# A graph network's gathered rows: the sums of pairs in a tile of their own instead of in place

## The chip, the cores and the metric

One Trainium2 chip, one core of it. The metric is the device time of one execution in microseconds (us); an execution takes about 4.4 ms, so that 0.3% are 13 us. The engines are TensorE (PE for matmuls, PEld for its weight loads), VectorE (DVE), ScalarE (ACT), GpSimd (POOL) and SyncE (SP). The engines run side by side, each through its own list of instructions in order, and wait for one another through semaphores.

## The reference, cut to what matters

Two graph networks follow each other on 3125 nodes and 103125 edges, in float32. The second has three attention layers of 256, 256 and 128 features, and only in these does the change act:

```python
def _gat(x, src, dst, W, a_src, a_dst, bias, n_nodes):
    H, C = a_src.shape
    xw = (x @ W).reshape(n_nodes, H, C)
    al_s = jnp.einsum('nhc,hc->nh', xw, a_src)
    al_d = jnp.einsum('nhc,hc->nh', xw, a_dst)
    logits = jax.nn.leaky_relu(al_s[src] + al_d[dst], LRELU_SLOPE)
    m = jax.lax.stop_gradient(jax.ops.segment_max(logits, dst, num_segments=n_nodes))
    e = jnp.exp(logits - m[dst])
    denom = jax.ops.segment_sum(e, dst, num_segments=n_nodes)
    alpha = e / denom[dst]
    out = jax.ops.segment_sum(alpha[:, :, None] * xw[src], dst, num_segments=n_nodes)
    return out.reshape(n_nodes, H * C) + bias
```

Each node sums the feature rows of its neighbours, each row weighted for each of the H = 8 heads.

## The kernel before

A search at the start sorts a node's edges into two kinds. Part of them is met by one-hot matrices (at most one edge for each block of 125 source nodes), the rest by gathering rows from a table in memory with indirect DMAs. For one attention layer `gat` first projects the features (L1107) and writes the table `tab`. Then `add_edges` sums over the edges, and `close_rows` joins both kinds of sums, normalizes and applies the activation. `add_edges` is written under a manual schedule: every engine takes its instructions in the order in which the Python code issues them, and nothing is reordered.

Its main loop goes over NT = 25 tiles of nodes. In pass `t` it works on two tiles at once, with two streams of edges.

The one-hot stream. For tile `t + 1`, `gather` (L1146) issues PE matmuls that look rows up with the one-hot matrix `hot` (L1152), two lookups to a PSUM pair `g`, of which there are two; ACT copies each pair to SBUF (L1153) and calls `pump()`. For tile `t`, `add_part` (L1190) multiplies the rows with the weights on DVE (`times`, L1188), adds the second half of the rows to the first on DVE (L1195), and PE sums the rest in PSUM with matmuls against the identity (L1197). ACT copies the sum out (L1303). `weigh` (L1174) makes the weights of the next tile from L1178 to the sum in `exps` (L1326), with the exponential on ACT (L1325).

The stream of gathered rows. A tile `t` has MORE[t] columns of gathered edges, one row for each of its 128 nodes in each column: 44 in the first tile, then 24, 22, 21, 20, 19, 18, 17, 17 and so on down to 7. The generator `fetches` fetches them column by column (L1021, an indirect DMA that POOL issues) into tiles `rows` of up to SG = 8 columns, a group each, with BUFS = 6 buffers. It is driven by `pump`: each ACT copy of a lookup pair lets one or two fetches go, and before the first of them ACT writes a few bytes into the row (L1221), which holds POOL back until ACT is there. `sum_others` takes a tile whose rows have been fetched long enough ago: `weigh_others` (L1255) makes its weights, again with the exponential on ACT, and `add_others` (L1266) sums it. In `add_others` DVE weights a group (L1188), adds its second half to its first, in place (L1272), and PE sums what is left in PSUM (L1274). With an odd number of columns the middle one is left as it is. ACT copies the sum out (L1280), and POOL scatters it to memory later (L1013).

In one pass the order on DVE is therefore: the two large parts of `add_part`, the logits of `weigh_others` and its exponential's sum, the small third part (`last`), the groups of `add_others`, and `weigh` for the next tile. Of the tile pools that matter here, `io` has two buffers for a name unless `bufs` says otherwise.

Of the kernel before, what the change touches and what calls it, by code (L numbers as in the profile page):

```python
# [10 lines left out]
F32 = mybir.dt.float32  # L11
# [8 lines left out]
P = 128  # L20
# [25 lines left out]
MORE = (44, 24, 22, 21, 20, 19, 18, 17, 17, 16, 16, 15, 15, 14, 14, 13, 13, 13, 12, 11, 11, 10, 10, 8, 7)  # L46
# [5 lines left out]
SG = 8  # L52
# [570 lines left out]
class Fast(Base):  # L623
# [510 lines left out]
    def add_edges(self, io, ps, layer, D, xt, yt, xw, ald, stat, tab, ald_d, res, more):  # L1134

        nc = self.nc
# [49 lines left out]
        def times(rows, e, s0, n):  # L1186
            r = rows[:, :n, :D].rearrange("p k (h c) -> p k h c", c=C)
            nc.vector.tensor_tensor(r, r, e[:, s0 : s0 + n, :, None].to_broadcast([*r.shape[:3], C]), op=ALU.mult)  # L1188
# [55 lines left out]
        def sum_others(ripe):  # L1244

            nonlocal held
            weighed = None
            while queue and queue[0][0] <= ripe:
                if weighed:
                    end_others(*add_others(*weighed))  # L1250
                weighed = weigh_others(*queue.pop(0)[1])
                held -= len(weighed[1])
            return weighed
# [12 lines left out]
        def add_others(t, groups, e, o):  # L1266
            pa = ps.tile([P, D], F32, name="pa2", tag="pa2")
            for rows, k0, n in groups:
                times(rows, e, k0, n)
                m = (n + 1) // 2  # L1270
                if n > 1:
                    nc.vector.tensor_add(rows[:, : n - m, :D], rows[:, : n - m, :D], rows[:, m:n, :D])  # L1272
                for k in range(m):
                    nc.tensor.matmul(  # L1274
                        pa, self.ident, rows[:, k, :D], start=k0 + k == 0, stop=k0 + n == MORE[t] and k == m - 1
                    )
            return t, o, pa

# [11 lines left out]
        for t in range(NT):  # L1290
            ahead = t + 1 < NT
            if t + 2 < NT:
                load(t + 2)
            nxt = parts(t + 1) if ahead else []
            pa = ps.tile([P, D], F32, name="pa1", tag="pa1")[:Q]
            for i in range(3):
                if ahead:
                    gather(t + 1, *nxt[i])
                if i == 2:
                    weighed = sum_others(copies - 8)  # L1300
                add_part(pa, e, *now[i])
            o = io.tile([P, D], F32, name="o1")[:Q]
            nc.scalar.copy(o, pa)  # L1303
            by_rows(nc.scalar, res[t * Q : (t + 1) * Q], o)
            added = weighed and add_others(*weighed)
            if ahead:
                now, e = nxt, weigh(t + 1, nxt)
            if added:
                end_others(*added)
        while queue or fetching.gi_frame:  # L1310
            for i in range(2 * SG):
                send(False)
            weighed = sum_others(copies)
            if weighed:
                end_others(*add_others(*weighed))
# [183 lines left out]
```

## Time and profile before

| | us |
|---|---|
| runs, median of 3 | 4444.06 |
| runs, lowest and highest | 4442.77, 4454.39 |
| the profiled execution | 4467.44 |
| its span, first to last instruction | 4465.6 |
| DVE products of gathered rows (L1188, `rows`) | 293.1 busy, x180 |
| POOL gathers (L1021, `rows`) | 1252.5 busy, x1200 |
| PE lookups (L1152, `hot`) | 584.8 busy, x2400 |

The page of a profile counts, for each engine, busy time, its share of the span and the instructions. A group line names line, engine, operation, what is written and what is read, the shapes (partitions x elements), the count, then busy time, mean ns of one, and the idle time of the engine just before such instructions with what ended most of it. A float32 matmul of this kernel stands in the trace as two passes, so that counts of PE are twice those in the code. The granted TensorE clock of the profiled execution was 0.753 of full speed on average. In the timeline a row is start, length, engine, line, operation, and in brackets the idle time before it and what ended that.

### The profile page before, as it was taken

The numbers are of one execution on the slowest core, as the hardware profiler recorded it, in microseconds if no ns is written. First come the engines' busy times: TensorE is split into PE (matmuls) and PEld (weight loads), VectorE is DVE, ScalarE is ACT, GpSimd is POOL, SyncE is SP. The second block draws the span as 40 slices with busy tenths as digits, with TensorE's granted clock in tenths as the row PEclk, the third lists the DMA queues.
The fourth block names the chain that finished last, engine by engine and source line by source line (L and its number), as shares of the span: only waits on it lengthen the run. The fifth ranks groups of instructions, "written<-read, shape, count | busy, mean of one in ns | idle before, by whom it ended". The sixth has DMA issues, their size and how long they took to land. (4 is left out here: it accounts for less than half of the span.)

```text
span 4465.6 us, 33146 instructions
## 1 busy us (share of the span) xinstructions
PE 2415.4 (54%) x10021; PEld 1730.4 (39%) x10021; DVE 2197.9 (49%) x3553; ACT 941.2 (21%) x2618; POOL 2002.9 (45%) x1916
## 2 busy tenths in 40 slices
PE   0001620000499767777777577777776555555545
PEld 0000300000133345565555445555555444444445
DVE  6898842100000227767666436666765434434445
ACT  0001620000000232232222332222232322121112
POOL 4415056777200045576652045567662045565550
PEclk8555955555799878888888788888888776776676
DMA  3001869500599463444331463344341553333322
GB/s 115 12 11 38 286 169 267 165 0 1 202 358 366 175 168 119 122 129 141 119 107 44 123 173 110 116 122 149 120 120 33 126 116 97 85 88 93 87 68 58
DMA packets 224527, 558.02 MB, mean 125 GB/s; under 512 B 89262, under 2 KB 134710, under 8 KB 208496
## 3 DMA queue, kind: packets, MB, share of 16 engines
q1 hardware_dynamic: 112286, 307.88, 20.7%
q0 software_dynamic: 74800, 158.73, 14.9%
q10 hardware_dynamic: 37250, 89.18, 6.6%
q8 instruction: 82, 1.34, 0.1%
q14 instruction: 109, 0.89, 0.1%
HBM read 439.37 MB, written 116.25 MB: 124 GB/s over the span
## 5 line engine op out<-in xcount | busy, mean ns | idle before, releaser
L1021 POOL DMA_INDIRECT rows<-tab,idx x1200 | 1252.5, 1044 | 894.1 <-ACT rows L1221 396.2
L1152 PE MATMUL g<-xw,hot 125*125 125x264 f32 (+1 forms) x2400 | 584.8, 394 | 252.9 <-issue 142.2
L1153 ACT COPY xt<-g 125x528 f32<-125x528 f32 (+1 forms) x900 | 474.5, 530 | 795.5 <-PE g L1152 411.7
L1152 PEld LDWEIGHTS g<-xw,hot 125*125 125x125 f32 x2400 | 434.6, 212 | 380.4 <-issue 169.7
L1013 POOL DMA_INDIRECT adj<-val,celli x400 | 423.9, 1060 | 299.8 <-DMA x<-in_x 148.4
L1049 PE MATMUL pa<-adj_t,h 125*64 125x500 f32 (+1 forms) x1050 | 270.7, 552 | 511.8 <-DMA adj_t<-adj 511.1
L1274 PE MATMUL pa<-rows,ident 128*128 128x256 f32 (+1 forms) x1236 | 391.8, 495 | 204.8 <-DVE rows L1272 163.3
L1021 POOL DMA_INDIRECT at<-ald,perm x75 | 78.2, 1043 | 789.2 <-DMA gat_dense<-dense 438.7
L1188 DVE TENSOR_TENSOR xt<-xt,le 125x3072 f32<-125x3072 f32 (+1 forms) x150 | 421.8, 2812 | 0.0
L1274 PEld LDWEIGHTS pa<-rows,ident 128*128 128x128 f32 x1236 | 304.4, 288 | 295.3 <-DVE rows L1272 197.4
L1197 PE MATMUL pa<-xt,ident 125*125 125x256 f32 (+1 forms) x1800 | 385.6, 369 | 39.1 <-DVE xt L1195 37.6
L1326 DVE TENSOR_REDUCE o<-le 128x8 f32<-128x104 f32 (+16 forms) x75 | 21.9, 292 | 740.1 <-ACT le L1325 484.4
L1152 PE MATMUL g<-xw,xt 125*125 125x264 f32 (+1 forms) x1350 | 319.8, 389 | 122.3 <-ACT xt L1153 62.0
L1197 PEld LDWEIGHTS pa<-xt,ident 125*125 125x125 f32 x1800 | 323.8, 209 | 90.8 <-DVE xt L1195 26.3
L1049 PEld LDWEIGHTS pa<-adj_t,h 125*64 125x64 f32 x1050 | 86.2, 136 | 675.5 <-issue 578.1
L170 DVE TENSOR_TENSOR h<-p,L_gnn_b 125x256 f32<-125x256 f32 (+1 forms) x21 | 8.3, 396 | 649.6 <-PE p L168 649.6
L1152 PEld LDWEIGHTS g<-xw,xt 125*125 125x125 f32 x1350 | 240.4, 211 | 189.6 <-ACT xt L1153 96.7
L1188 DVE TENSOR_TENSOR rows<-rows,le 128x2048 f32<-128x2048 f32 (+8 forms) x180 | 293.1, 1629 | 0.0
L1195 DVE TENSOR_TENSOR xt<-xt 125x1536 f32<-125x1536 f32 (+1 forms) x150 | 223.7, 1491 | 4.9
L1197 PE MATMUL pa<-last,ident 125*125 125x256 f32 (+1 forms) x300 | 92.9, 444 | 207.4 <-DVE last L1188 167.9
L1061 ACT COPY gin_acc<-pa 128x500 f32<-128x500 f32 (+1 forms) x21 | 10.2, 532 | 771.9 <-DMA adj_t<-adj 524.0
L1272 DVE TENSOR_TENSOR rows<-rows 128x1024 f32<-128x1024 f32 (+5 forms) x174 | 157.0, 902 | 6.0
(272 smaller groups left out, 2838.0 us busy)
## 6 DMA issues: line engine op xcount, KB each, us to landing
hot<-hot SPq DMA_DIRECT2D x48, 1562.5 KB
adj_t<-adj SPq DMA_DIRECT2D x144, 500.0 KB
adj_t<-adj SPq DMA_DIRECT2D x72, 562.5 KB
xt<-hot SPq DMA_DIRECT2D x24, 1562.5 KB
adj<-a ACTq DMA_DIRECT2D x25, 1367.2 KB
hot<-one ACTq DMA_DIRECT2D x25, 1367.2 KB
rows<-tab,idx POOLq DMA_INDIRECT x1200
row<-lane_d SPq DMA_DIRECT2D x25, 683.6 KB
```

Of the source, the lines that this page charges most:

```text
L1013: st = self.nc.gpsimd.indirect_dma_start(out=table, out_offset=bass.IndirectOffsetOnAxis(ap=idx, axis=0), in_=row, in_offset=None)
L1021: self.nc.gpsimd.indirect_dma_start(out=out, out_offset=None, in_=table, in_offset=bass.IndirectOffsetOnAxis(ap=idx, axis=0))
L1049: nc.tensor.matmul(pa[i * D0 : (i + 1) * D0, c // B, :w], h[:, s], tiles[i][:, c : c + w], start=s0 == 0, stop=s0 + i >= NT - 2 and i == 1,)
L1061: nc.scalar.copy(acc[:, :w], pa[:, c // B, :w])
L1152: nc.tensor.matmul(g[:Q, j, :W], one, xw[:, t if s == NT else s], start=True, stop=True)
L1153: nc.scalar.copy(rows[:, i : i + 2], g[:Q, :, :W])
L1188: nc.vector.tensor_tensor(r, r, e[:, s0 : s0 + n, :, None].to_broadcast([*r.shape[:3], C]), op=ALU.mult)
L1195: nc.vector.tensor_add(rows[:, :m, :D], rows[:, :m, :D], rows[:, m:n, :D])
L1197: nc.tensor.matmul(pa, self.ident[:Q, :Q], rows[:, j, :D], start=s0 + j == 0, stop=s0 + n == NS and j == m - 1)
L1272: nc.vector.tensor_add(rows[:, : n - m, :D], rows[:, : n - m, :D], rows[:, m:n, :D])
L1274: nc.tensor.matmul(pa, self.ident, rows[:, k, :D], start=k0 + k == 0, stop=k0 + n == MORE[t] and k == m - 1)
L1326: nc.vector.reduce_sum(den, e.rearrange("p k h -> p h k"), axis=AX.X)
```

## The change

The sum of pairs goes to a new tile `two` of SG // 2 = 4 columns, and PE reads `two` instead of `rows`. Where a group has an odd number of columns, the one that has no partner is copied to `two` by DVE. `two` is taken from `io`, which gives it two buffers; it has 4 x 256 x 4 = 4096 bytes in each partition for a layer of 256 features.

```diff
             for rows, k0, n in groups:
                 times(rows, e, k0, n)
                 m = (n + 1) // 2
+                two = io.tile([P, SG // 2, D], F32, name="two")
                 if n > 1:
-                    nc.vector.tensor_add(rows[:, : n - m, :D], rows[:, : n - m, :D], rows[:, m:n, :D])
+                    nc.vector.tensor_add(two[:, : n - m], rows[:, : n - m, :D], rows[:, m:n, :D])
+                if n % 2:
+                    nc.vector.tensor_copy(two[:, m - 1], rows[:, m - 1, :D])
                 for k in range(m):
                     nc.tensor.matmul(
-                        pa, self.ident, rows[:, k, :D], start=k0 + k == 0, stop=k0 + n == MORE[t] and k == m - 1
+                        pa, self.ident, two[:, k], start=k0 + k == 0, stop=k0 + n == MORE[t] and k == m - 1
                     )
             return t, o, pa
```

In the program that is built from it, no engine's order changes apart from the 36 copies that DVE gets. The sums on DVE from the third group of a layer on carry a wait for PE, and the first fetch into a reused `rows` buffer waits for DVE where it waited for DVE and PE.

## The prediction

> **What bounds the kernel now.** I read the page first, then the busy time by stretch, the waits, the answers for lines 1272, 1274 and 1021, and last the timeline of one pass of the loop over `t`. The edit sits in `add_others`, which runs only inside `add_edges`: three stretches of the span, about 1600 to 2455 us, 2560 to 3400 us and 3600 to 4380 us.
>
> ```profile
> 1600.00:2455.00 855.00, 638.00 (x2380) 482.25 (x2379) 561.28 (x663) 243.59 (x681) 483.95 (x447) 0.84 0.40 114
> 2560.00:3400.00 840.00, 633.39 (x2332) 470.62 (x2331) 522.57 (x616) 245.34 (x684) 487.39 (x448) 0.86 0.43 125
> 3600.00:4380.00 780.00, 426.54 (x2288) 380.40 (x2288) 340.07 (x630) 159.18 (x655) 417.77 (x433) 0.71 0.33 83
> ```
>
> The columns after the length are PE, PEld, DVE, ACT and POOL busy. No engine is full: PE 75% in the first two stretches and 55% in the third, DVE 66, 62 and 44%, POOL 54 to 58%. So the time is a loop of handovers, and the question is which handover comes last.
>
> ```profile
> DVE o L1326 <- ACT le L1325: 484.4, 41, 23.8
> POOL rows L1021 <- ACT rows L1221: 396.2, 128, 40.0
> PE pa L1274 <- DVE rows L1272: 163.3, 67, 15.4
> DVE lle L1258 <- DMA rows<-tab,idx: 48.8, 7, 13.6
> ```
>
> These are waits (total us, times, longest). DVE's big wait is for the exponential of the gathered edges, which ACT takes behind its copies of PE's lookups; PE in turn waits for DVE's sums. DVE waits for gathered rows hardly at all: seven times named so, all on `lle`, which is tile 0 of a layer, where no `rows` buffer has been used before. One pass, with 19 gathered rows (groups of 8, 8 and 3), shows the loop:
>
> ```profile
> 1909.83 0.32 DVE L1326 TENSOR_REDUCE o<-le 128x8 f32<-128x152 f32 x1 [5.69 <-issue]
> ...
> 1914.25 6.78 PE L1274 MATMUL pa<-rows,ident 128*128 128x256 f32 x20 [2.33 <-DVE rows L1272]
> 1916.43 1.23 DVE L1272 TENSOR_TENSOR rows<-rows 128x1024 f32<-128x1024 f32 x1
> 1917.58 0.95 DVE L1188 TENSOR_TENSOR rows<-rows,le 128x768 f32<-128x768 f32 x1
> ...
> 1918.56 0.42 DVE L1272 TENSOR_TENSOR rows<-rows 128x256 f32<-128x256 f32 x1
> 1918.90 0.56 DVE L1178 TENSOR_TENSOR le<-xt,ald 125x96 f32<-125x96 f32 x2
> ...
> 1925.81 1.76 DVE L1195 TENSOR_TENSOR xt<-xt 125x1536 f32<-125x1536 f32 x1
> ...
> 1927.63 2.85 PE L1197 MATMUL pa<-xt,ident 125*125 125x256 f32 x12 [0.79 <-DVE xt L1195]
> ```
>
> From 1909.83 to 1927.6 DVE runs almost without a gap (0.40 us for one exponential), and at the end PE waits 0.79 us for it. Before 1909.83 DVE idled 5.69 us. So DVE time added between the sums and L1195 reaches PE in such a pass; in passes where PE is later, the next exponential wait swallows it.
>
> **The change, part by part.**
>
> *Removed: POOL's wait for PE.* Refilling a `rows` buffer now waits for DVE's sum or copy instead of PE's matmuls. What that wait costs is in the answer for line 1274:
>
> ```profile
> who waited for it (us, times):
> ...
>   POOL rows L1021: 16.8, 6
> ```
>
> 6 times, 16.8 us of 4465.6. And the rows fetched earlier are not awaited: after tile 1 of a layer DVE never waits for them. Tile 1's late gathers are not helped, because the first fetch into a reused buffer stands behind an ACT copy (L1221, at 1699.86 us) that ACT runs after L1280, which itself needs all of tile 0's matmuls. Value: 0; bounds 0 and -17 us. I take 0.
>
> *Moved: the output of L1272, and PE's operand.* The 174 sums keep their lengths (1226 ns for 1024 elements); only the destination differs, and is now contiguous. PE runs the same 1236 passes. In the program each of these matmuls waited for the DMA semaphore of its own row; now one wait on DVE a group is left, two where a copy follows. That is free already: in the trace the start-to-start of L1274's passes inside a group is 216 ns at full granted clock and 427 ns at half, exactly that of L1197, which has no such waits. Value 0.
>
> *Added: 36 DVE copies.* Groups of odd length: 12 of the 25 tiles end in one (21, 19, 17, 17, 15, 15, 13, 13, 13, 11, 11, 7 rows), times three layers; 24 copies of 256 elements and 12 of 128. No such copy is in the trace. From below: the 8-element copy of L1109, 167 ns. From above: the two-input sum of 256 elements (L1272, 425 ns) and of 128 (290 ns). The 3125-element one-input row (L1377, 1850 ns) runs at under 0.6 ns an element, so I put 0.53 ns an element on the 167: 300 ns and 235 ns. Sum: 24 x 0.300 + 12 x 0.235 = 10.0 us of DVE (bounds 6.0 and 13.7). Behind each copy stand `weigh(t+1)` and the products of L1188 and L1195, and PE waits for L1195. PE's own wait for the copied row is covered: that matmul is the tile's last, and 2 to 8 passes of 216 to 427 ns from earlier rows or groups are still running. Looking through the 36 places, PE next waits for L1195 within 12 us in about 10, all in the first two layers; there the 0.30 us goes on the path, 3 us. In the third layer DVE idles up to 23.8 us for the next exponential, which covers its copies.
>
> A rule speaks against these copies. The Trainium skill, "SBUF — State Buffer", section "Who interferes with whom", says that an fp32 SBUF-to-SBUF copy takes DVE's second port pair, shared with GpSimd, as an exclusive lock, and that whichever of the two comes second is blocked outright. POOL is issuing gathers (949 ns each) more than half of the time. By the rule a copy could wait up to one issue: 36 x 0.95 = 34 us at most. The nearest rows say less: L1007, a one-input DVE operation, ran from 588 to 843 us while POOL issued scatters (L1013, 579.6 to 1153.9 us), and its 25 took 1830/1850/2048 ns (min/median/max), against 1850 for the same length at L1377 with POOL idle. So at most 0.2 us on one copy, about 0 at the median. I take the row. The other direction, POOL behind a copy, is at most 0.3 us a copy on a queue that nobody is late for.
>
> *Added: DVE waits for PE.* `two` has two buffers, so each sum from the third group on waits until PE has summed the group two before. Across tiles this is long past, since PE must have finished the old tile before the lookups that feed the next exponential. Within a tile it matters from three groups on: 12 waits a layer, 36 in all. In the pass above PE starts group 1 at 1914.25; eight passes at half clock (427 ns) and a drain of 0.6 us end near 1917.9, and the third sum would start at 1918.56: margin 0.6 us. With a third group of one row (17 rows, six tiles) DVE is ready 3.8 us after PE starts, PE needs about 3.6 to 4.0: margin about 0. Going through all 36, the modelled matmul ends give negative margins of under 0.1 us in three places; semaphore records, which are incomplete, would allow some 8 us in all. I take 2 us on the path, bounds 0 and 8. Queued behind such a wait is again `weigh(t+1)`.
>
> Sum: 3 + 2 = +5 us, on 4467.4 for the profiled execution (span 4465.6), so 4472. The median of the runs, 4444.06, lies 23 us below the profiled one; the same 5 us give 4449. I put no factor on the difference.
>
> **Rivals.**
>
> *The ring of two becomes the wait (slower).* One mechanism: the third sum of a tile stands behind PE, and DVE with it. For: margins near zero, and PE is at half clock in most of L1274 (median matmul 421 ns, the shortest 274). Against: the waits that I could place are short. It decides from about 0.4 us a wait: 36 x 0.4 = 14 us when most are on the path. With all copies exposed too: 10 + 10 = +20, 4464 us.
>
> *Earlier gathers pay (faster).* If POOL's 16.8 us were on the path: 4444 - 17 = 4427 us. For: rows are released some 2.4 us earlier on average (an estimate: the end of PE's last pass of a group less the end of its sum). Against: no DVE wait for rows after tile 1.
>
> *It does nothing that counts.* POOL is paced by ACT's copies (396.2 us of waits) and by its own issue, not by PE; all 10 us of copies fall into exponential waits: 4444 us. It would read as no change too.
>
> **How the numbers follow.** Forecast, +0 to +13 us: 0.62, likeliest 4449. Nothing that counts, within some us of 4444: 0.12. The ring: 0.20. Earlier gathers: 0.06. The kernel's runs spread from 4442.8 to 4454.4, and 0.3%, 13.3 us, is about what a measurement of it can tell from no change. Low end 4437: the gather case, 0.06, lies below it. High end 4464, the ring's full price; what is beyond it, with the gather case, is less than 0.2. The first two layers do the same work in passes of differing lengths, but from the second copy of L1303 in a layer to its last they take 777 and 780 us, so I add nothing for chance reshuffling.
>
> **What would show it.** Copies of about 300 and 235 ns, 36 of them; if one takes over 0.5 us with POOL busy, the port rule holds. DVE before the new sum waiting for PE on the matmul line: under 3 us in all is my case, over 14 us the ring's. POOL's waits for PE's sums gone, with POOL's waits for ACT unchanged. PE's wait for L1195 up from 37.6 us by about 5. I am wrong if a stretch shrinks by more than 10 us, or if DVE's exponential waits don't absorb the copies of the third layer.

## The result, and the profile after

The changed kernel takes 4468.58 us (median of 20 runs, 4426.66 to 4490.33) where the kernel before, run beside it, takes 4442.84 us (20 runs, 4415.16 to 4457.47): a ratio of 1.0054, 95% interval 1.0036 to 1.0073, or +24 us (+16 to +32). It is slower, and the time lies above the predicted range of 4437 to 4464.

The profiled execution took 4472.63 us (span 4470.8), against 4467.44 before. Two single executions 5 us apart cannot show a difference of 24 us between medians: the runs of the two kernels spread over 42 and 64 us. So the traces are read here for what the edit does, and the size comes from the repeated runs.

The three stretches in the changed kernel's busy time, columns as before:

```profile
1600.00:2455.00 855.00, 650.64 (x2412) 489.49 (x2412) 564.59 (x676) 247.97 (x694) 485.23 (x450) 0.85 0.41 117
2560.00:3400.00 840.00, 634.84 (x2333) 470.70 (x2332) 525.87 (x630) 244.61 (x684) 487.75 (x448) 0.86 0.43 125
3600.00:4380.00 780.00, 424.12 (x2265) 375.36 (x2265) 335.74 (x637) 157.76 (x652) 415.39 (x432) 0.70 0.32 82
```

No stretch stands out; in the third, DVE got through 4 us less of its work than before. The lines of the changed kernel are three further down from L1274 on: the sum is L1273, the copy L1275, the matmul L1277, the exponential's sum L1329. The groups of sums and copies, with the idle time of DVE ahead of them behind the bar, the sum before first:

```profile
L1272 DVE TENSOR_TENSOR rows<-rows 128x1024 f32<-128x1024 f32 (+5 forms) x174 | 157.0, 902 | 6.0
...
L1273 DVE TENSOR_TENSOR two<-rows 128x1024 f32<-128x1024 f32 (+5 forms) x174 | 157.1, 903 | 24.8 <-remote 7.8 <-issue 0.5
L1275 DVE COPY two<-rows 128x256 f32<-128x256 f32 (+1 forms) x36 | 10.0, 278 | 8.5 <-remote 7.4 <-PE pa L1277 0.7
```

The sum itself costs what it did. Its idle time rose from 6.0 us to 24.8 us, and 8.5 us lie ahead of the copies. Two things make that up. The answers for lines 1273 and 1275 have the first:

```profile
L1273 DVEq EVENT_SEMAPHORE  x156: 21/21/21, 1691.3 to 4373.6; - x156
...
L1275 DVE COPY two<-rows x36: 219/286/501, 1866.0 to 4374.2; 128x256 f32<-128x256 f32 x24, 128x128 f32<-128x128 f32 x12
```

A sum that waits both for its product and for PE gets an instruction of its own for the second wait, between the product and the sum. Before, a sum began 34 ns (median) after its product ended; with that instruction between, 104 ns. 156 x 70 ns = 10.9 us of DVE.

The second is real waiting for PE: 2.5 and 5.3 us before two sums, 7.4 and 0.7 us before two copies, 15.9 us in all. (`remote` says that no instruction ended near the signal that the profile could name; the semaphore that these four wait for is raised by PE alone. The 0.5 us before one more sum are left out: the profile names no signal for them, and a like gap stands below in a kernel with a ring of four, put down to DVE's own product.) The longest, in the timeline (DVE and PE rows):

```profile
3940.86 4.00 PE L1277 MATMUL pa<-two,ident 128*128 128x128 f32 x16 [0.71 <-DVE two L1273]
...
3942.64 0.28 DVE L1188 TENSOR_TENSOR rows<-rows,le 128x128 f32<-128x128 f32 x1
3950.31 0.23 DVE L1275 COPY two<-rows 128x128 f32<-128x128 f32 x1 [7.39 <-remote]
...
3950.59 0.80 PE L1277 MATMUL pa<-two,ident 128*128 128x128 f32 x2 [5.74 <-issue]
```

PE's records of the earlier groups end at 3944.86, but DVE is let go at 3950.31 only. In between PE has no record. Whether its passes ended later than the trace models them, or only their signal came late, the trace doesn't tell; below, a stall of PE is such a gap. Before, DVE would have gone on to L1178 in that time. Now it stands in the queue behind PE, and PE's last two passes in turn wait for the copy.

### The profile page after: what moved, and what is told of

Same layout as the page of the kernel before. It is cut to its first block, busy times and chain, and to the rows that moved or that the text cites. A ratio compares the mean times of both kernels' runs of the same rounds, so it can differ in the third digit from the quotient of the medians.

```text
span 4470.8 us, 33080 instructions
## 1 busy us (share of the span) xinstructions
PE 2422.1 (54%) x10021; PEld 1731.1 (39%) x10021; DVE 2204.9 (49%) x3589; ACT 938.5 (21%) x2618; POOL 1998.5 (45%) x1916
## 5 line engine op out<-in xcount | busy, mean ns | idle before, releaser
L1021 POOL DMA_INDIRECT rows<-tab,idx x1200 | 1249.9, 1042 | 882.6 <-ACT rows L1221 495.6
L1152 PE MATMUL g<-xw,hot 125*125 125x264 f32 (+1 forms) x2400 | 582.6, 392 | 233.7 <-issue 131.4
L1152 PEld LDWEIGHTS g<-xw,hot 125*125 125x125 f32 x2400 | 429.4, 210 | 363.6 <-issue 162.1
L1277 PE MATMUL pa<-two,ident 128*128 128x256 f32 (+1 forms) x1236 | 388.6, 490 | 224.3 <-DVE two L1273 197.6
L1188 DVE TENSOR_TENSOR xt<-xt,le 125x3072 f32<-125x3072 f32 (+1 forms) x150 | 421.8, 2812 | 0.0
L1277 PEld LDWEIGHTS pa<-two,ident 128*128 128x128 f32 x1236 | 299.7, 284 | 314.5 <-DVE two L1273 208.8
L1197 PE MATMUL pa<-xt,ident 125*125 125x256 f32 (+1 forms) x1800 | 393.8, 375 | 43.3 <-DVE xt L1195 42.5
L1152 PE MATMUL g<-xw,xt 125*125 125x264 f32 (+1 forms) x1350 | 324.6, 393 | 116.7 <-ACT xt L1153 48.9
L1329 DVE TENSOR_REDUCE o<-le 128x8 f32<-128x104 f32 (+16 forms) x75 | 21.9, 291 | 697.8 <-ACT le L1328 413.1
L1152 PEld LDWEIGHTS g<-xw,xt 125*125 125x125 f32 x1350 | 244.6, 213 | 185.3 <-ACT xt L1153 80.2
L1188 DVE TENSOR_TENSOR rows<-rows,le 128x2048 f32<-128x2048 f32 (+8 forms) x180 | 293.2, 1629 | 0.0
L1195 DVE TENSOR_TENSOR xt<-xt 125x1536 f32<-125x1536 f32 (+1 forms) x150 | 223.7, 1491 | 4.9
L1273 DVE TENSOR_TENSOR two<-rows 128x1024 f32<-128x1024 f32 (+5 forms) x174 | 157.1, 903 | 24.8 <-remote 7.8
```

The source lines that it names most:

```text
L1021: self.nc.gpsimd.indirect_dma_start(out=out, out_offset=None, in_=table, in_offset=bass.IndirectOffsetOnAxis(ap=idx, axis=0))
L1152: nc.tensor.matmul(g[:Q, j, :W], one, xw[:, t if s == NT else s], start=True, stop=True)
L1195: nc.vector.tensor_add(rows[:, :m, :D], rows[:, :m, :D], rows[:, m:n, :D])
L1197: nc.tensor.matmul(pa, self.ident[:Q, :Q], rows[:, j, :D], start=s0 + j == 0, stop=s0 + n == NS and j == m - 1)
L1273: nc.vector.tensor_add(two[:, : n - m], rows[:, : n - m, :D], rows[:, m:n, :D])
L1277: nc.tensor.matmul(pa, self.ident, two[:, k], start=k0 + k == 0, stop=k0 + n == MORE[t] and k == m - 1)
```

## The experiments

**Two sorts of chip.** The runs fell on several chips. In the runs of the result and in two later rows of runs the kernel before took 4442.84, 4442.09 and 4430.05 us; in three rows it took 4120.64, 4135.34 and 4125.23 us. I call the first sort A, the second B. One kernel, the changed one, in two profiles, on A and then on B, by the lookups and the exponential's waits:

```profile
L1152 PE MATMUL g<-xw,hot 125*125 125x264 f32 (+1 forms) x2400 | 582.6, 392 | 233.7 <-issue 131.4 <-ACT xt L1153 68.8 <-ACT last L1153 31.0
...
DVE o L1329 <- ACT le L1328: 413.1, 41, 22.7
```

```profile
L1152 PE MATMUL g<-xw,hot 125*125 125x264 f32 (+1 forms) x2400 | 513.1, 363 | 27.1 <-ACT xt L1153 25.7
...
DVE o L1329 <- ACT le L1328: 257.8, 75, 7.2
```

On A, PE stands still for 233.7 us ahead of the lookups, 131.4 us of it without any reason that the profile shows; on B for 27.1 us, every wait with its releaser. The mean granted clock was 0.754 and 0.775. Gaps of over 1 us in PE's records from 1600 to 4400 us, with no releaser to be found, number 72 in the changed kernel's trace on A and make 205.5 us; in the ten traces from A there are 59 to 72 of them, 148 to 206 us, and in the ten from B not one. So B has no such stalls of PE, and the runs spread over 9 to 23 us there, so it is the better place to see what the edit itself costs; A is where the result was measured. B is not simply A without stalls, though: in the same trace from B, DVE waits for gathered rows 35 times, 226.3 us in all, on A 7 times, 37.0 us. What stalls PE on A I could not find; of the 65 gaps in the trace of before, 34 stand at the same place in PE's order of instructions in the changed kernel's trace.

My theories before the first of these runs: (1) the ring of two makes DVE stand behind PE; (2) the separate wait instruction, 70 ns for each of 156 sums; (3) the copies; (4) gathers that start earlier and collide with the lookups' transfers.

| kernel | A: ratio to before [95%] | B: ratio to before [95%] |
|---|---|---|
| the change | 1.0054 [1.0036, 1.0073] | 1.0025 [1.0016, 1.0033]; 1.0016 [1.0007, 1.0025] |
| before + copies | 1.0023 [0.9996, 1.0050]; 1.0033 [1.0016, 1.0051] | not run |
| change, no copies | 1.0051 [1.0027, 1.0074]; 1.0044 [1.0023, 1.0065] | 0.9993 [0.9982, 1.0003] |
| change, ring of four | 1.0024 [1.0005, 1.0043]; 1.0018 [1.0003, 1.0034] | not run |
| no copies, ring of four | not run | 0.9998 [0.9990, 1.0007]; 1.0003 [0.9993, 1.0013]; 1.0005 [0.9996, 1.0013] |
| change, ring of one | not run | 1.0300 [1.0286, 1.0313] |
| products to a ring of two | 1.0077 [1.0049, 1.0105]; 1.0070 [1.0044, 1.0095] | not run |
| before, seven `rows` | not run | 1.0002 [0.9994, 1.0010]; 0.9997 [0.9988, 1.0006]; 1.0007 [0.9998, 1.0016] |

The chip of a row of runs could not be chosen, so some cells are empty.

**The change once more** (after_again, after_3), to have it beside others on one chip.

> The changed kernel once more, on one chip with the next three. Every theory: 20 to 28 us above the kernel before (4463 to 4470). It gives the mark for the other three in this row of runs; if it lay within 10 us of the kernel before, the 24 us of the first comparison would be mostly chance of the chip, and all theories would have to be cut down.

> The changed kernel, for a comparison on the same chip as the next three. On a chip of about 4440 us for the kernel before: 20 to 28 us slower than it. On a chip of about 4120 us: 9 to 11 us slower.

4130.77 us against 4120.64, and 4141.83 against 4135.34: +10.1 and +6.5 us on B, not 24. So there are two losses: one everywhere, and one on A alone.

**The copies alone** (before_copies, copies_2).

```diff
                     nc.vector.tensor_add(rows[:, : n - m, :D], rows[:, : n - m, :D], rows[:, m:n, :D])
+                if n % 2:
+                    spare = io.tile([P, D], F32, name="spare")
+                    nc.vector.tensor_copy(spare, rows[:, m - 1, :D])
```

> The kernel before, with the 36 copies alone, into a tile that nobody reads. Copy theory: +15 to +24 us. Wait-gap and ring theories: the copies are 286 ns each less an overlap of 84 ns with the sum before, 7 us of DVE, of which a part is on the path: +2 to +7 us.

> The kernel before with the 36 copies of odd columns into a tile that nothing reads; once more, for a tighter figure. On a chip where the kernel before takes about 4120 us and the changed kernel 10 us more, all or nearly all of these 10 us should be the copies, if VectorE's added work is what is left where TensorE does not stall: 8 to 11 us slower. If the ring of two or the gap ahead of the sums is what is left, 0 to 3 us slower. On a chip where the kernel before takes about 4440 us: 8 to 11 us slower as well.

Both on A: 4451.52 against 4442.09 and 4444.83 against 4430.05 us, +9 and +15. The first interval touches no change, the second does not. The copies make 9.6 us of DVE's records (copies_2's trace); as each starts about 84 ns before the sum ahead of it ends, they push what follows back by 7.3 us in all. For that the time grew by some 10 us: the copies count about in full, not at 3 us.

**The change without the copies** (nocopy, nocopy_2, nocopy_3): PE reads the odd column from `rows`.

```diff
-                if n % 2:
-                    nc.vector.tensor_copy(two[:, m - 1], rows[:, m - 1, :D])
...
-                        pa, self.ident, two[:, k], start=k0 + k == 0, stop=k0 + n == MORE[t] and k == m - 1
+                        pa, self.ident, two[:, k] if k < n - m else rows[:, k, :D], start=k0 + k == 0, stop=k0 + n == MORE[t] and k == m - 1
```

> The column without a partner is read by TensorE from the gathered rows, as before; no copies; the ring of two and the two waits stay. Wait-gap theory: +10 to +16 us, 156 sums start 104 ns after the product. Ring theory: +20, the long waits for PE are as in the changed kernel, except where the copy itself waited. Copy theory: 0 to +5 us.

> The change without the copies, ring of two; once more. On a chip of about 4120 us, where VectorE hardly ever waited for TensorE before a sum: 0 to 3 us slower than before, if the copies carry the 10 us there; 7 to 10 us slower, if it is the gap of 104 ns ahead of 155 sums. On a chip of about 4440 us: 10 to 20 us slower again, by long waits of VectorE for TensorE.

> The change without the copies, ring of two. On a chip of about 4440 us: 14 to 24 us slower than before (two comparisons gave 21 and 20), by the ring's waits. On a chip of about 4120 us, where there are hardly any such waits: 0 to 3 us slower if the copies were the 10 us there; 7 to 10 us if the gap ahead of 155 sums was.

On B 4131.51 against 4135.34: no loss, at most +1.2 us, although 156 sums still have the separate wait instruction (the answer for line 1273 lists it x156 again). The change itself took 10.3 us longer than this in the same row of runs. On B, then, the copies are the loss and the gaps ahead of the sums are not. On A it lost 21 and 24 us between the medians. In DVE's rows what stands out between the two is waiting for PE. The sums' group of nocopy_2 (A):

```profile
L1273 DVE TENSOR_TENSOR two<-rows 128x1024 f32<-128x1024 f32 (+5 forms) x174 | 157.1, 903 | 28.4 <-remote 11.7
```

In nocopy_3 (B) no wait for PE is named before a sum at all. The copies' place in the loop shows when the profiles of one row of runs on B are set side by side, by the time from the first to the last copy of `add_part`'s sum (L1303 before, three further down in the change) in each layer. Before stands as rows7_2, whose time is that of before (below):

| us | layer 1 | layer 2 | layer 3 |
|---|---|---|---|
| rows7_2 | 750.4 | 746.6 | 617.6 |
| nocopy_3 | 751.0 | 746.8 | 616.8 |
| after_3 | 754.0 | 750.5 | 615.9 |

The change adds 3.0 and 3.7 us to nocopy_3 in the first two layers, where 24 copies take 7.8 us, and nothing in the third. These are single executions; on another B chip after_again takes 4.2 and 3.9 us more than nocopy_ring4 (below) in the first two layers, and 3.5 us less in the third.

**A ring of four** (ring4, ring4_2), copies kept.

```diff
-                two = io.tile([P, SG // 2, D], F32, name="two")
+                two = io.tile([P, SG // 2, D], F32, name="two", bufs=4)
```

> The tile of sums with four buffers in place of two; all else as in the changed kernel (1.0054 of the kernel before, +24 us). Wait-gap theory (each sum that waits for two semaphores, DVE's own and PE's, starts 104 ns after the product before it in place of 34 ns; 156 sums carry it in the changed kernel): here 93 sums are left with two waits, so about 6.5 us of gap in place of 10.9, and no real wait for PE; the time falls by little, to +12 to +18 us. Ring theory (the three long waits for PE, 2.5, 5.3 and 7.4 us, and smaller ones are what counts): the time falls to +5 us or less. Copy theory (36 copies are what counts): unchanged at +24.

> The change with four tiles of sums, copies kept; once more. On a chip of about 4120 us: 8 to 11 us slower than before, so no better than the change itself (+10), since the ring has no long waits to give back there and the copies stay; 0 to 4 us slower, if it is the gap that costs. On a chip of about 4440 us: 8 to 11 us slower again.

4451.29 against 4442.09 and 4441.33 against 4430.05: +9 and +11 us on A, as with the copies alone (+9 and +15 beside it). The first lies between what two theories had said (5 or less, 12 to 18). Its groups (ring4_2):

```profile
L1273 DVE TENSOR_TENSOR two<-rows 128x1024 f32<-128x1024 f32 (+5 forms) x174 | 157.0, 902 | 12.4 <-DVE rows L1188 0.5
L1275 DVE COPY two<-rows 128x256 f32<-128x256 f32 (+1 forms) x36 | 10.4, 288 | 0.6
```

No wait for PE is left. It carries the copies, and yet it took 11.5 and 12.3 us less than nocopy and nocopy_2, which ran beside it on the same two chips without copies and with a ring of two. So on A the ring of two costs more than the copies do. The gap ahead of 87 sums is still there; it costs at most 87 x 70 ns = 6.1 us, and the 69 gaps that are gone can be at most 4.8 of the 12 us.

This run also bears on theory (4). It releases `rows` as early as the change does, it has the sum's new place and the copies, and it took no longer than the copies alone on the same two chips. So the gathers' earlier start shows no cost of its own on A either.

**No copies and a ring of four** (nocopy_ring4, nocopy_ring4_2, nocopy_ring4_3): both edits above.

> The change without the copies (TensorE reads the odd column from the rows) and with a ring of four tiles in place of two. What is left of the change is the sum's other output, and the separate semaphore instruction ahead of about 90 of the 174 sums, at 70 ns each. Theory that the wait instruction's gap carries the loss: 6 us slower than before, and all of it on the path. Theory of the ring: 0 to 6 us slower, and 12 to 20 us faster than the same without copies on a ring of two (+21). Theory that the place of TensorE's operand itself costs time: 15 us or more slower.

> The change without the copies and with a ring of four. On a chip of about 4440 us: 0 to 4 us slower than before by the theory of the ring, so 15 us or more faster than the run before this one; 6 us slower if the gap of some 90 sums counts in full; 15 us or more slower if the sum's new place costs by itself. On a chip of about 4120 us: within 3 us of before, as it was (+1).

> The change without the copies and with a ring of four, for a chip of about 4440 us: 0 to 4 us slower than before by the theory of the ring; 6 us slower if the gap of some 90 sums counts in full; 15 us or more slower, like the same on a ring of two (+21 and +24 between the medians), if the sum's new place costs by itself. On a chip of about 4130 us: no change, as it was twice.

Three times on B: +0.9, +1.1 and +0.6 us, every interval across no change. The sum's new place, PE's new operand and some 80 gaps cost nothing measurable there. It did not run on A.

**A ring of one** (ring1), `bufs=1` in the same place.

> The change with one tile of sums in place of two: every sum waits until TensorE has read the last group's sums. Theory of the ring: the waits of VectorE before the sums become common, 0.5 to 2 us each before most of the 174 sums, and the time goes up by much more than the change itself brought: 4520 to 4700 us. Theory of the wait instruction's gap (104 ns in place of 34 ns before each sum, whatever the ring): no more than the changed kernel, 4463 to 4475 us. Theory that VectorE's waits here are idle time that costs nothing, because the path runs through TensorE and the lookups: the waits come, and the time stays within 15 us of the changed kernel.

4244.97 against 4120.64: +124 us. The answer for line 1273 of its trace:

```profile
L1273 DVEq EVENT_SEMAPHORE  x165: 21/21/21, 1678.3 to 4146.2; - x165
its engine sat idle before it (us, times) until:
  PE pa L1277: 151.9, 93
```

With 13.9 us before the copies, DVE stood 165.8 us behind PE. On average that is 0.7 us of time for each us of waiting, once the copies' 8 us (the change's mean loss on B) are off. But the layers differ; rows7 (below, the time of before) ran on the same chip:

| us | layer 1 | layer 2 | layer 3 |
|---|---|---|---|
| rows7, first to last copy as above | 747.5 | 743.3 | 616.9 |
| ring1, the same | 808.9 | 804.6 | 619.0 |
| DVE's waits for PE in ring1 | 62.7 | 61.1 | 42.1 |

In the first two layers each us of waiting costs about 0.9 us (some 3.5 us a layer taken off for the copies), in the third next to nothing. So the theory that DVE's waits here are idle time that costs nothing is out for two layers and holds for the third, on B; the wait instruction's gap as the main cause is out too. What a long wait costs on A, where all three of the change stand in the third layer, this run does not show.

**The products elsewhere** (prod, prod_2): L1188 writes a ring of two tiles of eight columns, the sum is in place in them, and PE reads them. No copies, and no separate wait instruction.

```diff
-                times(rows, e, k0, n)
+                prod = io.tile([P, SG, D], F32, name="prod")
+                r = rows[:, :n, :D].rearrange("p k (h c) -> p k h c", c=C)
+                nc.vector.tensor_tensor(
+                    prod[:, :n].rearrange("p k (h c) -> p k h c", c=C), r,
+                    e[:, k0 : k0 + n, :, None].to_broadcast([*r.shape[:3], C]), op=ALU.mult
+                )
...
-                    nc.vector.tensor_add(rows[:, : n - m, :D], rows[:, : n - m, :D], rows[:, m:n, :D])
+                    nc.vector.tensor_add(prod[:, : n - m], prod[:, : n - m], prod[:, m:n])
...
-                        pa, self.ident, rows[:, k, :D], start=k0 + k == 0, stop=k0 + n == MORE[t] and k == m - 1
+                        pa, self.ident, prod[:, k], start=k0 + k == 0, stop=k0 + n == MORE[t] and k == m - 1
```

> The products go to a ring of two tiles of their own, the sum of pairs stays in place in it, TensorE reads it: no copies; the wait for PE is the only wait of the product, so no separate semaphore instruction stands before it; the gathered rows come free still earlier. Wait-gap theory: no gap of 104 ns anywhere, so 0 to +5 us, unless the product, which now waits for the group two before, waits for long (0.4 us for each third group at half clock: 36 x 0.4 = 14 us at most). Ring theory: +15 us or more, as the product stands further ahead of the sum and so waits longer. Copy theory: 0. If early release of the rows were what costs (gathers moved to a worse place), this one would be as slow as the changed kernel or slower, without any DVE waits.

> Products into a ring of two tiles, the sum in place in them, TensorE reads them: no copies and no separate semaphore instruction, but the ring's wait falls to the product, one instruction earlier than the sum. Once more. On a chip of about 4120 us: 0 to 6 us slower than before (some 20 waits of 0.2 to 0.4 us, no long ones) by the theory of the ring; 15 us or more, if putting the products elsewhere costs something by itself. On a chip of about 4440 us: 25 to 35 us slower again.

The slowest on A, +30 and +34 us, without a copy and with sums 34 ns behind their products. What it has is the ring's wait, one instruction earlier (prod_2):

```profile
L1271 DVE TENSOR_TENSOR prod<-rows,le 128x2048 f32<-128x2048 f32 (+8 forms) x180 | 293.1, 1629 | 20.0 <-remote 11.2 <-PE pa L1279 7.1 <-issue 1.6
...
3802.64 0.82 DVE L1271 TENSOR_TENSOR prod<-rows,le 128x640 f32<-128x640 f32 x1 [4.79 <-remote]
```

It points to the ring, but 19.9 us of waits cannot make 34 us of loss by themselves; it also frees `rows` one instruction earlier.

**The gathers' release alone** (rows7, rows7_2, rows7_3): the kernel before with one more `rows` buffer and the same limit on what is fetched.

```diff
-                    rows = io.tile([P, SG, W], F32, name="rows", bufs=BUFS)
+                    rows = io.tile([P, SG, W], F32, name="rows", bufs=BUFS + 1)
```

> The kernel before with seven tiles of rows in place of six: a gather then never waits for TensorE's reads of the tile of six groups ago, which is what the change brings for the gathers, and nothing else of the change is in it. Theory that the gathers moved forward cost the time (they meet the lookups' transfers): 10 to 25 us slower than before, and the changed kernel's loss is explained by it. Theory of the ring (VectorE stands behind TensorE): no change, within 5 us. A gain of 5 us or more would say that the release of the rows was worth something, and was covered up in the changed kernel.

> The kernel before with seven tiles of rows: the earlier release of the gathers and nothing else. On a chip of about 4440 us: no change within 6 us by the theory of the ring; 10 us or more slower, if the moved gathers make the 14 us that such a chip adds to the loss. On a chip of about 4120 us: no change, as it was.

> The kernel before with seven tiles of rows, for a chip of about 4440 us: no change within 6 us by the theory of the ring; 10 us or more slower if the moved gathers make the loss that such a chip adds. On a chip of about 4130 us: no change, as it was twice.

Three times on B: +0.7, -3.1 and +4.4 us between the medians, no interval clear of no change. POOL's release from PE is worth nothing there, and costs nothing. On A this kernel was not run; the ring of four is the evidence there.

None of these kernels beats the kernel before.

## Why the prediction was wrong

**The copies: the share on the path.** "Sum: 24 x 0.300 + 12 x 0.235 = 10.0 us of DVE" held: 286 and about 220 ns, 10.0 us in the trace. "PE next waits for L1195 within 12 us in about 10, all in the first two layers; there the 0.30 us goes on the path, 3 us" is the first step that failed. The loss on B, where the copies are all that counts, is 6.5 and 10.1 us; of the 24 copies in the first two layers nearly all are paid, not 10. The third layer's cover held on B: it did not grow. The prediction asked whether PE waits soon after each copy, when the loop as a whole, DVE to PE to ACT to DVE, carries a delay on to the next pass; that ring1 pays about 0.9 us for each us of waiting in these two layers fits this. The term was 3 us and measured about 8.

**The ring: the few long waits.** "I take 2 us on the path, bounds 0 and 8" is the second step that failed, on A. There a ring of two in place of four costs some 12 us or more (11.5 and 12.3 between the medians of the runs without copies and those with a ring of four, which carry the copies besides); on B, without copies, it costs nothing, and 2 us was near enough. The prediction went through 36 places with the matmul ends of one trace and looked for margins near zero. The waits came instead where PE stalled for microseconds: 15.2 us in three waits, all in the third layer. Stalls of that kind stood in the trace of before, as the 142.2 us with no other name than "issue":

```profile
L1152 PE MATMUL g<-xw,hot 125*125 125x264 f32 (+1 forms) x2400 | 584.8, 394 | 252.9 <-issue 142.2
```

That the long waits are what the ring costs on A is argued, not shown. Nor do the losses add up there: the copies alone cost 9 and 15 us, the ring without copies 21 and 24, both together 24 [16, 32].

**The rival of the ring** named the ring of two, which the ring of four bears out on A, and its sum (10 + 10, 4464) lies close to the 4468.58 measured. But it reckoned with 36 waits of 0.4 us, where the trace has three of 2.5 to 7.4 us, and its full price for all copies holds in two layers of three on B; that the sum came close is partly luck. Its chance of 0.20 was too low: it needed no small margins, only a PE that sometimes halts.

**POOL's release, value 0,** held: the waits for PE (16.8 us) are gone and the time didn't fall. Another 92.3 us of POOL's waits, named PE L1152 before, are gone with them, which the prediction did not count; POOL's wait for ACT (L1221), which I had expected unchanged, rose from 396.2 to 495.6 us instead. POOL's whole idle time ahead of these gathers fell only from 894.1 to 882.6 us. Rows7 gave no gain on B.

**The moved output and operand, value 0,** held on B (no copies, ring of four). What the step left out is the separate wait instruction, 10.9 us of DVE; on B this was free too.

**The port rule.** I took the row (at most 0.2 us a copy) over the Trainium skill's full blocking. The row told of DVE's side alone. In the changed kernel's first profile 12 copies overlap an indirect DMA of POOL's. With six of these the copy takes its usual time, but the gather ends 0.61 to 0.62 us after the copy, 1.08 to 1.44 us long where the median is 0.95:

```profile
2110.81 1.44 POOL L1021 DMA_INDIRECT rows<-tab,idx  x1 [0.30 <-issue]
2111.35 0.29 DVE L1275 COPY two<-rows 128x256 f32<-128x256 f32 x1
```

In two others the copy is the longer one, and ends 0.11 us after its gather. One such in after_3, in the timeline:

```profile
2914.27 1.95 POOL L1021 DMA_INDIRECT at<-ald,perm  x1 [0.30 <-issue]
...
2915.81 0.51 DVE L1275 COPY two<-rows 128x256 f32<-128x256 f32 x1
```

There are four of these in after_3, none in copies_2. So the blocking that "SBUF — State Buffer", section "Who interferes with whom", states is there, in both directions, and by the prediction's own sign (a copy of over 0.5 us) the port rule holds. It is cheap: DVE loses 0.2 us a time, under 1 us in all, close to the row's value; POOL loses up to 0.5 us a time, more than the 0.3 that I named, and about 1.5 us in all.

**PE's wait for L1195** rose from 37.6 to 42.5 us, the 5 that I named, while the time rose by 24: that one wait does not carry the sum. The match says little: the changed kernels without a copy have 38.5 to 41.2 us there on A.

**What stays open.** On A, that the ring of two makes the extra loss rests on the ring of four, which lacks it, and on B, which lacks both the loss and the waits; no run without copies and with a ring of four fell on A, and none with the copies alone on B. How the ring makes it is not shown, and the sizes don't close: without copies the visible waits are 5.4 and 11.7 us in two executions, for 21 and 24 us of loss, and prod loses more than its waits in full. Why 7 us of pushing back by the copies counts on B and 10.9 us of gaps ahead of the sums doesn't, on the same engine, is not settled either. And what stalls PE on A is not known.

## What to carry to other kernels

A tile of its own for a result that another engine reads puts the producer behind that reader: ask not only how the margins lie in an undisturbed pass, but what happens when the reader halts, and give the ring slack for that (here four buffers in place of two took back about 12 us on A). An engine that is half idle is not free in a loop of handovers; as a first estimate, price added work in full unless a wait in that very pass takes it up (the gaps ahead of the sums were an exception). And an effect of half a per cent can be two effects: run it on more than one chip before it gets one cause.

## What was unexpected in the hardware

- The same kernel took 4442.84 us on one chip and 4120.64 on another (8% apart), with PE's unexplained idle time ahead of the lookups 131.4 us on one and none on the other (the changed kernel's traces).
- A second wait of a DVE instruction stands in the trace as an instruction of its own, and the dependent sum starts 104 ns after its product in place of 34 ns.
- A DVE copy and an indirect DMA of POOL's hold each other up: of 12 pairs in one trace, the gather waited in six (up to 1.44 us long, median 0.95) and the copy in two (0.50 us, usually 0.29).
- A ring of one made DVE wait 62.7, 61.1 and 42.1 us for PE in the three layers, and their loops, with the copies, grew by 61, 61 and 2 us.
